# Six buffers for the terms of q, segment ends made in pieces, the first step's loads put ahead, and one-hots made three blocks ahead, in a graph attention layer

## The chip, the cores and the metric

The kernel runs on one core of a Trainium2 chip. A core has TensorE (PE; matmuls and transposes, with weight loads shown apart as PEld), VectorE (DVE), ScalarE (ACT), GpSimd (POOL) and SyncE (SP). SP computes nothing here and issues DMA transfers; POOL issues the indirect ones. Sixteen DMA engines move the data. The metric is the device time of one execution in microseconds; the time of the kernel before is 2341.86 us, the median of three runs (2341.75 to 2342.19).

## The reference

There are 12,500 nodes with 128 features, 212,500 edges sorted by destination, 8 heads of 16. Cut to what is computed:

```python
h = maximum(layernorm(x), 0)
q = h @ Wq.T + bq;  v = h @ Wv.T + bv          # of nodes
k = edge_attr @ Wk.T + bk                      # of edges
in_m   = sum over a head (q[src] * k)
out_m  = sum over a head (q[dst] * k)
diag_m = sum over a head (q[src] * q[dst])
score = (segsoftmax(in_m / 4, dst) + segsoftmax(out_m / 4, dst)
         + segsoftmax(diag_m / 4, dst)) * edge_weight ** lam
agg = segment_sum(score[..., None] * v[dst], dst)
out = x + leaky_relu(agg @ Wo.T + bo, 0.1)
```

## The kernel before

The function `ordered_path` does the work (`general_path` is skipped for these inputs). Edges are cut into blocks of `BE` = 512, and these into five streams of consecutive blocks (`S` = 5). A step `t` takes one block of each stream, so there are `T` = 84 steps and 420 blocks; block `g` is stream `g % 5` of step `g // 5`.

**The stage of the nodes** (0 to 155 us). For 25 groups of up to four tiles of 128 nodes, h is normalized, turned and multiplied by wq (`rectify`, `turn_h`, `nodes_q`), and q is stored to `q_table` in float32 by SP (line 833). Beside it the arrays of the edges are made: source indices (`edges_1`), flags of segment starts (`edges_2`), the position of each edge's destination relative to its block's first one (`edges_3`, `rel_b`, stored to `rel_d`) and the weight in three bf16 terms (`edges_4`), the flags and terms stored to `fa_d` by `fa_out` from the rotating tile `of`. Then POOL starts to gather rows of `q_table` by source index for the first nine blocks (`gather`, line 625, four gathers of 128 rows a block), SP loads the edge features of the first six blocks (`fetch_edges`, line 617), and `terms_q` splits q into three bf16 terms: for group g ACT copies the first term (line 845), DVE subtracts it (846), and one call later ACT makes the second (851), DVE the third (852), and SP stores the tile `q3` to `q3_table` (854). `q3` has three buffers. In the middle of these, after group 12, `edges_5` checks the order of the edges (line 756), marks the ends of segments (758) and turns them (707, 708).

**The loop over the blocks.** For a block the destination's q is not gathered. Edges are sorted, so the destinations of a block lie in a window of 42 nodes: SP loads the window's rows of `q3_table` (`win`, line 1054, an address from a register that SP has loaded from `bases`, 1049) and the relative positions, spread over 126 partitions (`relb`, 1044); ACT makes one-hots of them (`one_hots`, 1062 and 1063), and PE spreads the window's rows over the edges (`spread_q`, 1087). ACT copies the result beside the gathered rows (1089). Edge features are turned (`turn`, 1068 and 1070) and multiplied by wk (`project`, 1076 and 1078), and DVE forms products and sums (`logits`, 1097, 1098, 1100). Scans over the five streams together, in places 0 to 4 of the following steps, give running maxima and sums, from which finished nodes are computed between the blocks (`nodes_between`) or after the loop.

**What sets the order.** Nearly every instruction passes through `pin`, which ties it behind the instruction pinned last on the same engine: the order on an engine is the order of the program. `fetch(t)` loads what step t needs and is called at place 3 of step t - 2; `fetch(0)`, `fetch(1)` and the five one-hots of step 0 stand before the loop. A gather runs `LOOK` = 9 blocks ahead of the loop, into 11 buffers; from block 10 on it also waits for products of PE, by this part of `gather`:

```python
if (g - LOOK, j) in behind:
    tc.add_manual_dep(rows.ins, behind[g - LOOK, j], ...)   # j = 0: project(g - LOOK)
```

Edge features are loaded six blocks ahead into seven buffers, `relb` and `win` have two buffers, and the one-hots of a step one tile of five blocks, in two buffers.

Of the kernel before, what the change touches and what calls it, by code (L numbers as in the profile page):

```python
# [7 lines left out]
F32 = mybir.dt.float32  # L8
BF = mybir.dt.bfloat16
I32 = mybir.dt.int32  # L10
AF = mybir.ActivationFunctionType
# [461 lines left out]
def ordered_path(ctx: ExitStack, tc: tile.TileContext, flag, x, src, dst, edge_attr, edge_weight,  # L473
# [118 lines left out]
    def pin(inst):  # L592

        engine = str(inst.ins.engine)
        if engine in pinned:
            tc.add_manual_dep(inst.ins, pinned[engine], mybir.DependencyInfo(
                mybir.DependencyClass.NoSync, mybir.DependencyReason.DATA), reason="in order")
        pinned[engine] = inst.ins.name
        return inst
# [8 lines left out]
    qqs, st, eas, behind = {}, {}, {}, {}  # L608

    def fetch_edges(g):  # L610
        if g < S * T:
# [37 lines left out]
    with tc.tile_pool(name="prep", bufs=1) as prep, \  # L649
# [49 lines left out]
            nc.gpsimd.tensor_tensor(weight, weight, lam_sb.to_broadcast([RW, RC]), op=ALU.pow)  # L699


        def turn_edges(of, to):
            cols = of.rearrange("r (a p j) -> r a j p", a=RB, j=JN)
            for a in range(RB):
                t_ps = prep_ps.tile([P, JN, RW], F32, name="t_ps")
                for j in range(JN):
                    pin(nc.tensor.transpose(t_ps[:, j, :], cols[:, a, j, :], ident[:RW, :RW]))
                pin(nc.vector.tensor_copy(to[:, a:NB:RB, :], t_ps.rearrange("p j r -> p r j")))
# [8 lines left out]
                                  of.rearrange("r (a e) -> r a e", a=RB)))  # L717

        def of_tile():
            return prep.tile([RW, RC], BF, name="of", bufs=2)  # L720

        def edges_1():
            pin(nc.vector.tensor_copy(src_f, src_r))
# [10 lines left out]
        def edges_3():  # L734
            base_c = prep.tile([RW, RB], F32, name="base_c")
            pin(nc.vector.tensor_copy(base_c, dst_f[:, 1:RC + 1:BE]))
            for a in range(RB):
                part = rel[:, a * BE:(a + 1) * BE]
                pin(nc.vector.tensor_scalar(part, part, base_c[:, a:a + 1], 1.0, op0=ALU.subtract,
                                            op1=ALU.add))  # L740
            rel_b = prep.tile([RW, RB, BE], BF, name="rel_b")
            pin(nc.gpsimd.tensor_copy(rel_b.rearrange("r a (j p) -> r a j p", j=JN),
                                      rel.rearrange("r (a p j) -> r a j p", a=RB, j=JN)))
            pin(nc.sync.dma_start(rel_d.rearrange("(r a) e -> r a e", a=RB), rel_b))
# [5 lines left out]
                pin(nc.vector.tensor_sub(weight, weight, of))  # L750
            fa_out(c + 1, of)

        def edges_5():
            bad = got["bad"] = prep.tile([RW, 1], F32, name="bad")
            step = got["step"]
            pin(nc.vector.tensor_reduce(bad, step[:, :RC], AX.X, ALU.min))
            last = step[:, 1:]
            pin(nc.vector.scalar_tensor_tensor(last, last, 0.0, rel, op0=ALU.is_gt, op1=ALU.mult))
            turn_edges(last, ends)

        def turn_w(i, to):
            w_ps = prep_ps.tile([P, F], F32, name="t_ps")
# [76 lines left out]
        def terms_q(g):  # L839

            if g < GN:
                n = len(tiles_of(g))
                q = xq[:, g * JN:g * JN + n, :]
                q3 = q3s[g] = node.tile([P, JN, 3, F], BF, name="q3", bufs=3)[:, :n]
                pin(nc.scalar.copy(q3[:, :, 0, :], q))
                pin(nc.vector.tensor_sub(q, q, q3[:, :, 0, :]))
            if g > 0:
                n = len(tiles_of(g - 1))
                q = xq[:, (g - 1) * JN:(g - 1) * JN + n, :]
                q3 = q3s.pop(g - 1)  # L850
                pin(nc.scalar.copy(q3[:, :, 1, :], q))
                pin(nc.vector.tensor_sub(q3[:, :, 2, :], q, q3[:, :, 1, :]))
# [36 lines left out]
            gather(g)  # L889
        for g in range(AHEAD):  # L890
            fetch_edges(g)
        for g in range(GN + 1):
            terms_q(g)
            if g == GN // 2:
                edges_5()
        bad = got["bad"]

        found = prep.tile([1, 7], F32, name="found")
# [25 lines left out]
        nc.vector.tensor_copy(flag, found[:, 6:7])  # L924


    fin = ctx.enter_context(tc.tile_pool(name="fin", bufs=2))

    def unit_in(to, u):
# [9 lines left out]
    class Nodes:  # L939
# [88 lines left out]
    with tc.tile_pool(name="work", bufs=2) as work, \  # L1028
            tc.tile_pool(name="scan", bufs=2) as scan, \
            tc.tile_pool(name="ps", bufs=1, space=PSUM) as ps:  # L1030
        ks, eTs, qds, lTs, base_v = {}, {}, {}, {}, {}
        end = S * T

        def block_rows(t):
            lo = t if t < G else t - 1
            return lo, slice(0, S * G) if t < G else slice(1, S * G + 1)

        def fetch(t):

            if t >= T:  # L1040
                return
            at, part = block_rows(t)
            relb = load.tile([K3, S, BE], BF, name="relb")
            pin(nc.sync.dma_start(relb, rel_d[part].rearrange("(s b) e -> s b e", b=G)
                                  [None, :, at, :].to_broadcast([K3, S, BE])))
            fa = load.tile([4 * S, BE], BF, name="fa", bufs=4)
            for s in range(S):
                pin(nc.sync.dma_start(fa[4 * s:4 * s + 4], fa_d[s * G + t]))
            _, base_v[t] = nc.values_load_multi_w_load_instructions(
                bases[0:1, t, 0:S], engines=[mybir.EngineType.SP], min_val=0, max_val=N - 1,  # L1050
                skip_runtime_bounds_check_because="the indices of nodes are below N")
            win = load.tile([K3, S, F], BF, name="win")
            for s in range(S):
                pin(nc.sync.dma_start(win[:, s, :], q3_table[bass.ds(base_v[t][s] * 3, K3), :]))
            st[t] = dict(relb=relb, fa=fa, win=win)

        def one_hots(t, s):

            if s == 0:
                st[t]["oh"] = work.tile([K3, S, BE], BF, name="oh")  # L1060
            d = st[t]["relb"][:, s, :]
            pin(nc.scalar.activation(d, d, AF.Abs, bias=before[:K3]))  # L1062
            pin(nc.scalar.activation(st[t]["oh"][:, s, :], d, AF.Relu, bias=1.0, scale=-1.0))  # L1063

        def turn(g):
            eT_ps = ps.tile([P, JN, P], F32, name="eT_ps", bufs=2)
# [16 lines left out]
        def spread_q(g):  # L1083
            s, d = g % S, st[g // S]
            qd_ps = ps.tile([P, JN, F], F32, name="qd_ps")
            for j in range(JN):
                pin(nc.tensor.matmul(qd_ps[:, j, :], d["oh"][:, s, j * P:(j + 1) * P],  # L1087
                                     d["win"][:, s, :], start=(j == 0), stop=(j == JN - 1)))
            pin(nc.scalar.copy(qqs[g][:, :, 1, :], qd_ps))  # L1089
            qds[g] = qd_ps  # L1090

        def logits(g):
            s, t = g % S, g // S
# [142 lines left out]
                    r.normalize(0, 4)  # L1236

        products = str(mybir.EngineType.PE)
        fetch(0)
        fetch(1)  # L1240
        for s in range(S):
            one_hots(0, s)
        turn(0)
        turn(1)
        spread_q(0)
        project(0)
        for g in range(end + 2 * S):
            s, t = g % S, g // S
            if g < end:
                gather(g + LOOK)  # L1250
                fetch_edges(g + AHEAD)
            if g + 1 < end:
                project(g + 1)
                behind[g + 1, 0] = pinned[products]
                spread_q(g + 1)
            if g + 2 < end:
                turn(g + 2)
            if g < end:
                logits(g)
            if t + 1 < T:  # L1260
                one_hots(t + 1, s)
            if s == 0:
                later(turn_logits, t - 1)
                later(turn_sums, t - 2)
            elif s == 1:
                later(scan_max, t - 1)
            elif s == 2:
                later(to_rows, t - 2)
                later(powers, t - 1)
            elif s == 3:  # L1270
                later(scan_sums, t - 1)
                if t + 2 < T:
                    fetch(t + 2)
            else:
                later(select, t - 1)
                later(put_rows, t - 2)
            behind[g + 1, 2] = pinned[products]
# [72 lines left out]
```

## Time and profile before

| | |
|---|---|
| median of three runs | 2341.86 us |
| the profiled execution, its span | 2333.37 us, 2331.5 us |
| busy: PE, PEld, DVE, ACT, POOL | 78%, 61%, 92%, 65%, 71% of the span |
| gathers (L625, POOL) | 1680, 966 ns each in the mean |
| products and sums (L1097, L1098, L1100, DVE) | 420 each, 677, 1214 and 1753 ns |
| one-hots (L1062, L1063, ACT) | 420 each, 729 and 630 ns |
| first gather; first and last block's L1097 | 91.7; 169.8 and 2260.2 us |

The span is the time from the first instruction of the profiled execution to the last. Busy time leaves out what an engine spends on issue: a gather occupies POOL for its duration and the gap to the next one. In lists of waits a line gives the engine and line that waited, what ended the wait, the sum in us, how often, and the longest. In timelines the columns are start in us, duration in us, engine, line, operation, destination<-sources, shapes, count, and in brackets the engine's idle time before it with what ended that.

### The profile page before, as it was taken

What the parts mean: (1) busy time and instruction counts of PE and PEld (TensorE: products, weight loads), DVE (VectorE), ACT (ScalarE), POOL (GpSimd) and SP (SyncE); (2) the same over time, 40 slices, a digit from 0 to 9 for tenths busy, and PEclk for the clock granted to TensorE, in tenths of its full rate; (3) what the DMA queues carried; (4) which work ended last, traced back from release to release, by engine and by line L of the source; (5) the groups of instructions that cost most, each with busy time, mean ns of one, the idle gap of its engine ahead of it and who ended that gap; (6) DMA issues with size and microseconds to landing.
All of it is one profiled execution on the core that took longest, in us unless ns stands there. A gap on an engine that the chain in (4) does not pass through costs nothing. (4 is left out here: it accounts for less than half of the span.)

```text
span 2331.5 us, 35994 instructions
## 1 busy us (share of the span) xinstructions
PE 1812.6 (78%) x10629; PEld 1415.8 (61%) x10629; DVE 2150.8 (92%) x2263; ACT 1522.1 (65%) x2797; POOL 1658.1 (71%) x1715
## 2 busy tenths in 40 slices
PE   5327888888788888878878778888887777888775
PEld 4315666666666666666666566666666666666654
DVE  7659999999999999999999999999999999999983
ACT  5547676666766676666676676667666667667653
POOL 3547777777777777777777777777777777777740
PEclk9757777777778787787777787778687888688777
DMA  7657545555555555555555655554555554554522
GB/s 201 215 172 197 148 135 148 143 144 149 141 136 159 138 141 163 139 139 154 146 138 139 164 138 140 156 144 137 158 142 140 153 154 135 153 154 134 149 54 60
DMA packets 306681, 341.04 MB, mean 146 GB/s; under 512 B 137667, under 2 KB 225496, under 8 KB 306165
## 3 DMA queue, kind: packets, MB, share of 16 engines
q1 hardware_dynamic: 244906, 222.99, 32.5%
q0 software_dynamic: 54448, 112.96, 19.9%
q10 hardware_dynamic: 7120, 2.70, 0.4%
q8 instruction: 85, 1.39, 0.2%
q14 instruction: 122, 1.00, 0.1%
HBM read 307.79 MB, written 30.64 MB: 145 GB/s over the span
## 5 line engine op out<-in xcount | busy, mean ns | idle before, releaser
L625 POOL DMA_INDIRECT qq<-q_table,src_i x1680 | 1623.4, 966 | 548.6 <-issue 341.4
L1100 DVE TENSOR_REDUCE lT<-prod 128x96 f32<-128x1536 f32 x420 | 736.2, 1753 | 14.4
L1078 PE MATMUL k_ps<-wk,eT 128*128 128x128 f32 x3360 | 613.3, 338 | 103.6 <-ACT eT L1070 95.4
L1078 PEld LDWEIGHTS k_ps<-wk,eT 128*128 128x128 f32 x3360 | 518.9, 236 | 263.7 <-ACT eT L1070 180.9
L1089 ACT COPY qq<-qd_ps 128x512 f32<-128x512 f32 x420 | 245.4, 584 | 548.9 <-PE qd_ps L1087 432.2
L1098 DVE TENSOR_TENSOR prod<-qq,k_ps 128x1024 f32<-128x1024 f32 x420 | 509.8, 1214 | 0.5 <-PE k_ps L1078 0.5
L1087 PE MATMUL qd_ps<-win,oh 126*128 126x128 bf16 x1680 | 203.4, 257 | 213.4 <-DVE prod L1097 173.1
L1068 PE MATMUL eT_ps<-ident,ea 128*128 128x128 f32 x1680 | 342.0, 341 | 2.9 <-DVE found L901 2.9
L1097 DVE TENSOR_TENSOR prod<-qq,qd_ps 128x512 f32<-128x512 f32 x420 | 284.3, 677 | 47.4 <-ACT qq L1089 34.6
L1087 PEld LDWEIGHTS <-oh 126*128 126x128 bf16 x1680 | 159.5, 116 | 257.5 <-issue 208.4
L1062 ACT ACTIVATE relb<-relb,before 126x512 bf16<-126x512 bf16 x420 | 306.3, 729 | 7.4 <-DMA relb<-rel_d 7.4
L1070 ACT COPY eT<-eT_ps 128x512 f32<-128x512 f32 x420 | 246.9, 588 | 50.3 <-PE eT_ps L1068 48.7
L1063 ACT ACTIVATE oh<-relb 126x512 bf16<-126x512 bf16 x420 | 264.6, 630 | 13.4
L1068 PEld LDWEIGHTS eT_ps<-ident,ea 128*128 128x128 f32 x1680 | 243.0, 181 | 3.2 <-DVE found L901 3.2
L1178 PE MATMUL b_ps<-ident,sum 120*128 120x120 f32 x672 | 141.1, 342 | 94.8 <-ACT l L1120 92.3
L1076 PE MATMUL k_ps<-b,ones 3*128 3x512 bf16 x420 | 190.8, 454 | 5.0 <-DVE prod L1098 4.8
L1191 PE MATMUL w_ps<-back,sel 128*126 128x144 f32 x1344 | 186.9, 295 | 0.6 <-ACT back L1179 0.6
L1178 PEld LDWEIGHTS b_ps<-ident,sum 120*128 120x128 f32 x672 | 101.3, 215 | 138.6 <-ACT l L1120 111.4
L1191 PEld LDWEIGHTS w_ps<-back,sel 128*126 128x126 f32 x1344 | 178.4, 197 | 0.8 <-ACT back L1179 0.8
L1179 ACT COPY back<-b_ps 128x480 f32<-128x480 f32 x168 | 97.6, 581 | 47.0 <-PE b_ps L1178 47.0
L1130 DVE TENSOR_TENSOR_SCAN u<-l,u,far_ps 120x512 f32<-120x512 f32 x83 | 105.5, 1271 | 0.8 <-ACT l L1120 0.8
L1158 DVE TENSOR_TENSOR_SCAN sum<-keep,sum,up 120x512 f32<-120x512 f32 x83 | 105.9, 1276 | 0.0
(170 smaller groups left out, 1735.4 us busy)
## 6 DMA issues: line engine op xcount, KB each, us to landing
ea<-in_edge_attr_dram SPq DMA_DIRECT2D x419, 256.0 KB
relb<-rel_d SPq DMA_DIRECT2D x84, 630.0 KB
qq<-q_table,src_i POOLq DMA_INDIRECT x1680
win<-q_table SPq DMA_DIRECT2D x420, 31.5 KB
q_table<-q SPq DMA_DIRECT2D x24, 384.0 KB
fa<-fa_d SPq DMA_DIRECT2D x420, 4.0 KB
sums<-rows SPq DMA_DIRECT2D x416, 7.9 KB
q_table<-xq SPq DMA_DIRECT2D x24, 256.0 KB
```

Of the source, the lines that this page charges most:

```text
L625: rows = pin(nc.gpsimd.indirect_dma_start(out=qq[:, j, 0, :], out_offset=None, in_=q_table, in_offset=bass.IndirectOffsetOnAxis(ap=src_i[: ...
L1062: pin(nc.scalar.activation(d, d, AF.Abs, bias=before[:K3]))
L1063: pin(nc.scalar.activation(st[t]["oh"][:, s, :], d, AF.Relu, bias=1.0, scale=-1.0))
L1068: pin(nc.tensor.transpose(eT_ps[:, j, :], eas[g][:, j * F:(j + 1) * F], ident))
L1070: pin(nc.scalar.copy(eT, eT_ps))
L1078: pin(nc.tensor.matmul(k_ps[:, j, :], eTs[g][:, j, :], wk, start=False, stop=(j == JN - 1)))
L1087: pin(nc.tensor.matmul(qd_ps[:, j, :], d["oh"][:, s, j * P:(j + 1) * P], d["win"][:, s, :], start=(j == 0), stop=(j == JN - 1)))
L1089: pin(nc.scalar.copy(qqs[g][:, :, 1, :], qd_ps))
L1097: pin(nc.vector.tensor_mul(prod[:, :, 2, :], qqs[g][:, :, 0, :], qds[g]))
L1098: pin(nc.vector.tensor_mul(prod[:, :, 0:2, :], qqs[g], ks[g][:, :, None, :].to_broadcast([P, JN, 2, F])))
L1100: pin(nc.vector.tensor_reduce(lTs[t][:, :, s, :], prod.rearrange("p j i (h d) -> p j (i h) d", d=DIM), AX.X, ALU.add))
L1191: pin(nc.tensor.matmul(w_ps[:, i].rearrange("p s c -> p (s c)"), d["sel"][:, j, lo:lo + 3, :].rearrange("p s w -> p (s w)"), d["back"][:, ...
```

## The change

There are four parts. The tile `q3` gets six buffers: four of its own, and for every third group one of the two `of` tiles, for which `rel_b` becomes an `of` tile too. `edges_5` is cut into six pieces, one after every third call of `terms_q`. `fetch` is split: `fetch(t)` loads relb and fa and the registers, `fetch_rows(t)` the windows; both move up in the program, and `fetch(0)` is called before `terms_q`. The one-hots get a tile for each block, in five buffers; one block's are made at a time, three blocks ahead of the loop, and before the loop the first block's one-hots, turn, project and spread_q come ahead of the second block's turn.

```diff
+    def fetch(t):
...
+        relb = load.tile([K3, S, BE], BF, name="relb")
+        pin(nc.sync.dma_start(relb, rel_d[part].rearrange("(s b) e -> s b e", b=G)
+                              [None, :, at, :].to_broadcast([K3, S, BE])))
+        fa = load.tile([4 * S, BE], BF, name="fa", bufs=4)
+        for s in range(S):
+            pin(nc.sync.dma_start(fa[4 * s:4 * s + 4], fa_d[s * G + t]))
+        _, base_v[t] = nc.values_load_multi_w_load_instructions(
...
+    def fetch_rows(t):
...
+        win = st[t]["win"] = load.tile([K3, S, F], BF, name="win")
+        for s in range(S):
+            pin(nc.sync.dma_start(win[:, s, :], q3_table[bass.ds(base_v[t][s] * 3, K3), :]))
...
         def of_tile():
-            return prep.tile([RW, RC], BF, name="of", bufs=2)
+            return prep.tile([P, RC], BF, name="of", bufs=2)[:RW]
...
-            rel_b = prep.tile([RW, RB, BE], BF, name="rel_b")
+            rel_b = of_tile().rearrange("r (a e) -> r a e", a=RB)
...
-        def edges_5():
-            bad = got["bad"] = prep.tile([RW, 1], F32, name="bad")
+        def edges_5(i):
             step = got["step"]
-            pin(nc.vector.tensor_reduce(bad, step[:, :RC], AX.X, ALU.min))
             last = step[:, 1:]
-            pin(nc.vector.scalar_tensor_tensor(last, last, 0.0, rel, op0=ALU.is_gt, op1=ALU.mult))
-            turn_edges(last, ends)
+            if i == 0:
+                bad = got["bad"] = prep.tile([RW, 1], F32, name="bad")
+                pin(nc.vector.tensor_reduce(bad, step[:, :RC], AX.X, ALU.min))
+            elif i == 1:
+                pin(nc.vector.scalar_tensor_tensor(last, last, 0.0, rel, op0=ALU.is_gt,
+                                                   op1=ALU.mult))
+            elif i < 2 + RB:
+                turn_edges(last, ends, [i - 2])
...
-                q3 = q3s[g] = node.tile([P, JN, 3, F], BF, name="q3", bufs=3)[:, :n]
+                if g % 3 == 2:
+                    q3 = prep.tile([P, JN, 3, F], BF, name="q3", tag="of", bufs=2)
+                else:
+                    q3 = node.tile([P, JN, 3, F], BF, name="q3", bufs=4)
+                q3 = q3s[g] = q3[:, :n]
...
         for g in range(AHEAD):
             fetch_edges(g)
+        fetch(0)
         for g in range(GN + 1):
             terms_q(g)
-            if g == GN // 2:
-                edges_5()
+            if g % 3 == 2:
+                edges_5(g // 3)
...
-        def one_hots(t, s):
-
-            if s == 0:
-                st[t]["oh"] = work.tile([K3, S, BE], BF, name="oh")
-            d = st[t]["relb"][:, s, :]
-            pin(nc.scalar.activation(d, d, AF.Abs, bias=before[:K3]))
-            pin(nc.scalar.activation(st[t]["oh"][:, s, :], d, AF.Relu, bias=1.0, scale=-1.0))
+        def one_hots(g):
+
+            if g < end:
+                oh = ohs[g] = work.tile([K3, BE], BF, name="oh", bufs=5)
+                d = st[g // S]["relb"][:, g % S, :]
+                pin(nc.scalar.activation(d, d, AF.Abs, bias=before[:K3]))
+                pin(nc.scalar.activation(oh, d, AF.Relu, bias=1.0, scale=-1.0))
...
-        fetch(0)
+        fetch_rows(0)
         fetch(1)
-        for s in range(S):
-            one_hots(0, s)
+        fetch_rows(1)
+        one_hots(0)
         turn(0)
+        project(0)
+        spread_q(0)
         turn(1)
-        spread_q(0)
-        project(0)
+        one_hots(1)
+        one_hots(2)
...
-            if t + 1 < T:
-                one_hots(t + 1, s)
+            one_hots(g + 3)
...
-                if t + 2 < T:
-                    fetch(t + 2)
+                fetch(t + 2)
+                fetch_rows(t + 2)
```

More of the change, by code (lines that the diff above doesn't have):

```diff
@@ L606, in rows_in, with block_rows @@
         q.dma_start(to[RW - 1:RW, :E - top], t[None, top:E])
-    qqs, st, eas, behind = {}, {}, {}, {}
+    qqs, st, eas, behind, base_v = {}, {}, {}, {}, {}
+    def block_rows(t):
+        lo = t if t < G else t - 1
+        return lo, slice(0, S * G) if t < G else slice(1, S * G + 1)
+    def fetch(t):
+        if t >= T:
+            return
+        at, part = block_rows(t)
+        relb = load.tile([K3, S, BE], BF, name="relb")
[5 more added lines that the diff above has]
+        _, base_v[t] = nc.values_load_multi_w_load_instructions(
+            bases[0:1, t, 0:S], engines=[mybir.EngineType.SP], min_val=0, max_val=N - 1,
+            skip_runtime_bounds_check_because="the indices of nodes are below N")
+        st[t] = dict(relb=relb, fa=fa)
+    def fetch_rows(t):
+        if t >= T:
+            return
+        win = st[t]["win"] = load.tile([K3, S, F], BF, name="win")
+        for s in range(S):
+            pin(nc.sync.dma_start(win[:, s, :], q3_table[bass.ds(base_v[t][s] * 3, K3), :]))
     def fetch_edges(g):
@@ L699, in ordered_path, with turn_edges @@
             nc.gpsimd.tensor_tensor(weight, weight, lam_sb.to_broadcast([RW, RC]), op=ALU.pow)
-        def turn_edges(of, to):
+        def turn_edges(of, to, which=range(RB)):
             cols = of.rearrange("r (a p j) -> r a j p", a=RB, j=JN)
-            for a in range(RB):
+            for a in which:
                 t_ps = prep_ps.tile([P, JN, RW], F32, name="t_ps")
@@ L924, in ordered_path @@
         nc.vector.tensor_copy(flag, found[:, 6:7])
+    assert GN // 3 >= 2 + RB
     fin = ctx.enter_context(tc.tile_pool(name="fin", bufs=2))
@@ L1030, in ordered_path @@
             tc.tile_pool(name="ps", bufs=1, space=PSUM) as ps:
-        ks, eTs, qds, lTs, base_v = {}, {}, {}, {}, {}
+        ks, eTs, qds, ohs, lTs = {}, {}, {}, {}, {}
         end = S * T
[L1034 to L1046, printed above, removed]
-            for s in range(S):
[L1048 to L1055, printed above, removed]
-        def one_hots(t, s):
-            if s == 0:
-                st[t]["oh"] = work.tile([K3, S, BE], BF, name="oh")
-            d = st[t]["relb"][:, s, :]
-            pin(nc.scalar.activation(d, d, AF.Abs, bias=before[:K3]))
-            pin(nc.scalar.activation(st[t]["oh"][:, s, :], d, AF.Relu, bias=1.0, scale=-1.0))
+        def one_hots(g):
[4 more added lines that the diff above has]
+                pin(nc.scalar.activation(oh, d, AF.Relu, bias=1.0, scale=-1.0))
         def turn(g):
@@ L1086, in spread_q @@
             for j in range(JN):
-                pin(nc.tensor.matmul(qd_ps[:, j, :], d["oh"][:, s, j * P:(j + 1) * P],
+                pin(nc.tensor.matmul(qd_ps[:, j, :], ohs[g][:, j * P:(j + 1) * P],
                                      d["win"][:, s, :], start=(j == 0), stop=(j == JN - 1)))
@@ L1090, in spread_q @@
             qds[g] = qd_ps
+            del ohs[g]
         def logits(g):
@@ L1238, in ordered_path @@
         products = str(mybir.EngineType.PE)
-        fetch(0)
+        fetch_rows(0)
         fetch(1)
-        for s in range(S):
-            one_hots(0, s)
+        fetch_rows(1)
+        one_hots(0)
         turn(0)
+        project(0)
+        spread_q(0)
         turn(1)
-        spread_q(0)
-        project(0)
+        one_hots(1)
+        one_hots(2)
         for g in range(end + 2 * S):
```

## The prediction

> **What bounds the kernel now.** I read the page first, then the waits, then the timeline around the start and the end of the edge loop. The page's 40 slices (58.3 us each) suggest VectorE:
>
> ```profile
> DVE  7659999999999999999999999999999999999983
> POOL 3547777777777777777777777777777777777740
> DMA  7657545555555555555555655554555554554522
> ```
>
> From slice 4 on DVE is at nine tenths and POOL at seven. But the page counts no issue time, so the second view is the list of waits (engine and line, what it waited for: us in total, times, longest):
>
> ```profile
> POOL qq L625 <- issue: 341.4, 1120, 0.3
> ACT qq L1089 <- DMA qq<-q_table,src_i: 106.5, 61, 3.0
> POOL qq L625 <- PE k_ps L1078: 43.6, 58, 26.2
> ACT q L845 <- DMA q_table<-q: 33.8, 21, 8.4
> ```
>
> POOL never waits longer than 0.3 us before a gather, except once, 26.2 us; ACT, which copies the spread q into the same tile, waits 106.5 us for gathers. The timeline near the end of the loop shows who leads (start, us, engine, line):
>
> ```profile
> 2246.76 0.94 POOL L625 DMA_INDIRECT qq<-q_table,src_i  x1 [0.30 <-issue]
> 2250.24 0.68 DVE L1097 TENSOR_TENSOR prod<-qq,qd_ps 128x512 f32<-128x512 f32 x1
> 2251.40 0.58 ACT L1089 COPY qq<-qd_ps 128x512 f32<-128x512 f32 x1 [1.94 <-DMA qq<-q_table,src_i]
> 2251.76 0.94 POOL L625 DMA_INDIRECT qq<-q_table,src_i  x1 [0.30 <-issue]
> 2260.24 0.66 DVE L1097 TENSOR_TENSOR prod<-qq,qd_ps 128x512 f32<-128x512 f32 x1
> ```
>
> The last gather (block 419) is issued by 2252.70, and DVE uses it at 2260.24, 7.5 us later, though the program lets gathers run 9 blocks ahead. I subtracted, for each block, the end of its fourth gather from the start of its L1097. This lead is 33.9 us at block 10, 24.9 at 40, 10.0 at 90, and then stays between 5 and 12 to the end. Up to block 90 DVE works off the lead at 4.78 us a block (blocks 40 to 90); after that it goes at the pace of the gathers: 1640 gathers from 173.73 to 2252.70, each 1.268 us with its 0.30 us of issue, 5.07 us a block. **The loop ends when POOL's stream of gathers ends**, and the remaining 78.8 us (2331.5 - 2252.7) follow it. So the time is set by when that stream runs without a hole. Its one hole:
>
> ```profile
> 146.59 0.94 POOL L625 DMA_INDIRECT qq<-q_table,src_i  x1 [0.30 <-issue]
> 155.69 0.54 SPq L1044 DMA_DIRECT2D relb<-rel_d  x1
> 159.46 3.67 SPq L1054 DMA_DIRECT2D win<-q_table  x5
> 161.79 0.72 ACT L1062 ACTIVATE relb<-relb,before 126x512 bf16<-126x512 bf16 x1 [7.41 <-DMA relb<-rel_d]
> 168.84 2.08 PE L1078 MATMUL k_ps<-wk,eT 128*128 128x128 f32 x8 [4.42 <-ACT eT L1070]
> 171.38 2.08 PE L1078 MATMUL k_ps<-wk,eT 128*128 128x128 f32 x8
> 173.73 0.94 POOL L625 DMA_INDIRECT qq<-q_table,src_i  x1 [26.20 <-PE k_ps L1078]
> ```
>
> Forty gathers (blocks 0 to 9) are through at 147.53; gather 41 is tied to the products of block 1 (line 171.38), which come only after the terms of q are stored, the first step is loaded and its one-hots are made. A change here is worth at most 26.2 - 0.3 = 25.9 us, unless the first forty get quicker.
>
> **The terms of q (stores L854).** With three buffers the store of group g holds up L845 of group g + 3:
>
> ```profile
> 102.06 0.62 ACT L845 CAST q<-xq 128x512 bf16<-128x512 f32 x1 [2.04 <-DMA q_table<-q]
> 103.32 0.68 DVE L852 TENSOR_TENSOR q<-xq,q 128x512 bf16<-128x512 f32 x1
> 106.90 0.62 ACT L845 CAST q<-xq 128x512 bf16<-128x512 f32 x1 [1.94 <-DMA q_table<-q]
> ```
>
> L852 ends at 104.0, and its buffer is free at 106.9: a store takes 2.6 to 3.0 us to land in all such pairs. Groups 6 to 12 start 2.38 us apart (103.82 to 118.11), while DMA is only 0.68 busy (100 to 120). In the DMA records a store is 256 packets of 1536 bytes at 66 ns, over 16 engines 1.05 us; a gather is 16 packets at 280 ns, 0.28 us per 1.27. So two stores' latency, not bandwidth, sets this pace. Six buffers leave five stores in flight; then the slower of two limits holds: DMA, 1.05 / (1 - 0.22) = 1.35, and DVE, 0.61 + 0.69 = 1.30 us a group. I take 1.40.
>
> **The loads put ahead** (fetch(0): relb, five fa, the registers). On SP's queue they now stand between the six ea and the first store: 0.54 + 1.93 + 1.33 (the median of the register loads, L1049) = 3.8 us, so that store is issued at 95.3 instead of 91.54. In the DMA engines it also goes behind relb, 630 packets of 1024 bytes at 74 ns = 2.9 us. Before, the first store landed at 97.5; now about 100.5. Behind it waits ACT's L845 of group 6, and behind that everything of the later groups. This is a loss of 3 us on the stage, paid out of 18 gained below.
>
> **The ends in pieces.** Before, L756 (2.28), L758 (2.29) and four turns with copies (2.6, and waits for PE) stood together between 119.97 and 128.5 and starved the stores: DMA was at 0.17 between 124.5 and 129.5. The same instructions now come after groups 2, 5, 8, 11, 14 and 17. The first two fall before the first landing, when DVE has nothing else to do (groups 0 to 5 plus both end near 98); the four copies, 0.6 each, hide behind four queued stores. If that cover were gone they would cost their 7.2 us again.
>
> So the last store lands near 100.5 + 24 x 1.40 = 134, against some 158.4 before (issued 155.65, + 2.8).
>
> **From there to gather 41.** The order is new: one-hots of block 0 (0.72 + 0.63), copy of eT(0) 0.59, project(0) 2.08, spread_q(0) 0.64, copy of qq 0.60, the turn and copy of eT(1) about 1.0, bias and project(1) 2.7: 9 us if even the first one-hot must wait for the last store (its tile may lie in released memory; relb is there). The win loads take 2.5 us beside it. Queued behind these on ACT are one-hots 1 and 2, needed two blocks later; on SP, fetch(1), whose relb is first read in block 2. Project(1) ends near 143. Before, five pairs of one-hots (6.4 us) stood ahead of eT(0).
>
> **The forty gathers.** They end at 147.5, after 143. POOL is then the later one by 4.5 us, and gather 41 follows at 147.8: **25.9 us** earlier. The one operation that might delay them is the denser DVE work. One gather of the old stage is long:
>
> ```profile
> 122.28 2.29 DVE L758 SCALAR_TENSOR_TENSOR step<-step,dst_r 104x2048 f32<-104x2048 f32 x1
> 122.42 2.98 POOL L625 DMA_INDIRECT qq<-q_table,src_i  x1 [0.30 <-issue]
> ```
>
> It took 2.98 instead of 0.944 beside an instruction with two SBUF inputs. The Trainium skill ("SBUF — State Buffer", Who interferes with whom) says that such an instruction and a GpSimd one that reads SBUF exclude each other for a whole instruction. Taken for all of them (50 subtractions of 0.68 plus 2.29 = 36 us) the forty would end at 91.66 + 40 x 1.25 + 36 = 178, and the change would lose 4 us. But the same instructions ran beside the same gathers here: all forty together are 6.2 us over 0.944 each. I keep the row: between 0 and some 10 us over, 141 to 151 for the end.
>
> **The rotation of "of".** rel_b loses its own buffer, so the cast L748 that ran at 73.58 must wait for rel_d's store, issued at 69.37; the next such wait (78.83, for a store issued at 73.21) shows 5.6 us, so to 75.0. Behind it on DVE stand L750 and L832, behind these the last q_table stores and the first gather: 0 to 1.4 us; I take 0.4, since L832's sums have three PSUM tiles of slack.
>
> **One-hots in the loop** number the same, on ACT (65% busy), three blocks ahead instead of five. relb is needed at place 2 of the step before and its buffer is freed at place 1: six blocks, 30 us, for a load that took 6.1 us at the start. Cost 0; rival C prices the other end. The end of the loop and the nodes left over are unchanged.
>
> **Sum.** 25.9 - 0.4 = 25.5 us. The profiled execution took 2333.37 (span 2331.5) and would take 2307.9; the runs' median is 8.5 us above it, and I assume it stays so: 2341.86 - 25.5 = **2316 us**.
>
> **Rivals.**
> A (the forecast, 0.72): POOL's stream is whole; 22 to 29 us, 2313 to 2320.
> B (0.15): the stores don't speed up (receipts, not buffers, are the limit), and PE holds gather 41. At the old 2.38 us the last store lands at 100.5 + 24 x 2.38 = 157.6, project(1) ends at 166.6 and gather 41 starts at 166.9: 7 us, 2335. For it: a store needs 2.6 us with DMA only 0.68 busy. Against it: DMA at 1.02 in another stretch (180 to 195), so more in flight does move more. A pace between gives 2320 to 2335.
> C (0.05, slower): the later relb. If ACT waits for it at place 2 of each of 83 steps, the slack of DVE against POOL, (5.07 - 4.78) x 5 = 1.45 us a step, is used up first; from 1.45 + 25.5 / 83 = 1.76 us a step on the kernel is slower; at 2 us it is 83 x 0.55 - 25.5 = 20 us more, 2362. Against it: 24 of the 30 us would have to be lost.
> D (0.04): no change, within 0.2% (4.7 us, about what a measurement of this kernel can tell). A gather interval longer by 25.5 / 1640 = 16 ns would do it; 2342.
> E (0.04): the stage's delays of gathers (6.2 us) vanish too: up to 32 us, 2310.
>
> **The numbers.** Faster is A, B and E, 0.91; same 0.04; slower 0.05. The range 2311 to 2329 leaves out C, D, the far end of B and of E.
>
> **What would show it.** L845's wait falls from 33.8 us to near 10; stores start about 1.4 us apart; DMA near 0.9 from 95 to 134. POOL has no hole over 5 us; its last gather ends near 2227, and interval and final lead stay 1.268 and about 8 us. A hole before gather 41 means B; waits of ACT's L1062 on relb mean C. The forecast is wrong if gathers are not the bound, that is if their last one moves by 26 us and the end does not.

## The result and the profile after

The changed kernel takes **2318.68 us** (median of four runs, 2315.46 to 2320.5) against 2342.03 us (four runs, 2341.75 to 2345.21) for the kernel before: the ratio on record is 0.9895, with a 95% interval of 0.9881 to 0.991. The gain is 23.4 us by the medians; 2316 us and 25.5 us of gain were predicted. The profiled execution took 2320.5 us (span 2318.7), the longest of its four, while the profiled execution before was 8.4 us or more below the other runs of its kernel, so the two profiles differ by only 12.9 us. Nine of the twelve runs below came on chips where this program, before as after, takes some 2918 us: the instructions of VectorE, ScalarE and GpSimd have the same durations there, but in the loop pauses appear on every engine, many of which no row of the profile explains, and gathers come 1.60 us apart and stay 46 to 60 us ahead of their use.

Lines have moved: the gather is now L652, the terms of q are L880 to L889 (L880 and L881 the first term and its subtraction, L889 the store), the checks and marks of the ends L785 and L787, the one-hots L1076 and L1077, the products L1112 to L1115. The slices of the page (58.0 us each) look like those of before, but for the second and third, where all three rows are fuller (DMA 0.7 and 0.8 for 0.6 and 0.5; the third was where POOL and the stores had stood still):

```profile
DVE  6889999998999999999989999999999999999983
POOL 3677777777777777777777777777777777777750
DMA  7785555454554545555544555555455454545522
```

The list of waits (engine and line, what it waited for: us in total, times, longest):

```profile
POOL qq L652 <- issue: 321.2, 1053, 0.3
ACT qq L1103 <- DMA qq<-q_table,src_i: 76.6, 39, 4.3
DVE prod L1112 <- DMA qq<-q_table,src_i: 17.2, 16, 3.5
ACT q L880 <- DMA q_table<-q: 5.7, 1, 5.7
```

No wait over 0.3 us before a gather is left but that of the first, and L880 waits for a store once, 5.7 us, where L845 had waited 33.8 us. The second and third lines name the DMA landing that came last before a wait ended, and a landing of a later block's gather counts there too; so each wait has to be set against the landings of its own block. By the semaphores of the traces a gather has landed about 2 us after its instruction ends (the median). Counting only waits that ended within 0.3 us of the last landing of the block's own gathers, L1112 waits for gathers 11 times, 13.7 us in all; before the change this was so 3 times, 1.6 us. The timeline shows how the start went (start, us, engine, line; brackets: idle before it and what ended that):

```profile
93.40 7.44 POOL L652 DMA_INDIRECT qq<-q_table,src_i  x1 [10.77 <-DMA ea<-in_edge_attr_dram]
93.99 0.68 DVE L881 TENSOR_TENSOR xq<-xq,q 128x512 f32<-128x512 f32 x1
...
97.08 4.34 SPq L889 DMA_DIRECT2D q_table<-q  x4
97.60 2.28 DVE L787 SCALAR_TENSOR_TENSOR step<-step,dst_r 104x2048 f32<-104x2048 f32 x1
101.14 0.97 POOL L652 DMA_INDIRECT qq<-q_table,src_i  x1 [0.30 <-issue]
102.24 0.62 ACT L880 CAST q<-xq 128x512 bf16<-128x512 f32 x1 [5.71 <-DMA q_table<-q]
...
127.71 0.72 ACT L1076 ACTIVATE relb<-relb,before 126x512 bf16<-126x512 bf16 x1
133.05 2.51 SPq L635 DMA_DIRECT2D win<-q_table  x5
136.99 0.69 DVE L1112 TENSOR_TENSOR prod<-qq,qd_ps 128x512 f32<-128x512 f32 x1 [3.27 <-ACT qq L1103]
137.87 2.08 PE L1092 MATMUL k_ps<-wk,eT 128*128 128x128 f32 x8
151.11 0.94 POOL L652 DMA_INDIRECT qq<-q_table,src_i  x1 [0.30 <-DMA qq<-q_table,src_i]
152.36 0.94 POOL L652 DMA_INDIRECT qq<-q_table,src_i  x1 [0.30 <-PE k_ps L1092]
...
2241.05 0.94 POOL L652 DMA_INDIRECT qq<-q_table,src_i  x1 [0.30 <-issue]
2242.03 0.68 DVE L1112 TENSOR_TENSOR prod<-qq,qd_ps 128x512 f32<-128x512 f32 x1
...
2248.51 0.66 DVE L1112 TENSOR_TENSOR prod<-qq,qd_ps 128x512 f32<-128x512 f32 x1
```

The products of block 1 (137.87) are done 12 us before the fortieth gather ends (152.05), and gather 41 follows at 152.36 without a hole: POOL alone decides when it starts, 21.4 us earlier than before. The first L1112 comes 32.8 us earlier (136.99 for 169.79). But the last gather ends at 2241.99, only 10.7 us earlier. The 1640 gathers between have a mean interval of 1.2744 us instead of 1.2679, and 1640 x 6.5 ns = 10.7 us. The end of the loop follows 6.5 us behind the last gather (7.5 before).

### The profile page after: what moved, and what is told of

It reads as the page before. It is cut to its first block, busy times and chain, and to the rows that moved or that the text cites. A ratio compares the mean times of both kernels' runs of the same rounds, so it can differ in the third digit from the quotient of the medians.

```text
span 2318.7 us, 35998 instructions
## 1 busy us (share of the span) xinstructions
PE 1817.0 (78%) x10629; PEld 1416.8 (61%) x10629; DVE 2150.2 (93%) x2263; ACT 1523.5 (66%) x2797; POOL 1671.1 (72%) x1715
## 5 line engine op out<-in xcount | busy, mean ns | idle before, releaser
L652 POOL DMA_INDIRECT qq<-q_table,src_i x1680 | 1636.4, 974 | 523.0 <-issue 321.2
L1115 DVE TENSOR_REDUCE lT<-prod 128x96 f32<-128x1536 f32 x420 | 736.1, 1753 | 14.4
L1112 DVE TENSOR_TENSOR prod<-qq,qd_ps 128x512 f32<-128x512 f32 x420 | 284.3, 677 | 62.2 <-ACT qq L1103 41.0
L1076 ACT ACTIVATE relb<-relb,before 126x512 bf16<-126x512 bf16 x420 | 306.3, 729 | 0.0
L1077 ACT ACTIVATE oh<-relb 126x512 bf16<-126x512 bf16 x420 | 264.5, 630 | 17.6 <-DVE flag L960 4.2
```

Of the source, the lines that this page charges most:

```text
L652: rows = pin(nc.gpsimd.indirect_dma_start(out=qq[:, j, 0, :], out_offset=None, in_=q_table, in_offset=bass.IndirectOffsetOnAxis(ap=src_i[: ...
L1077: pin(nc.scalar.activation(oh, d, AF.Relu, bias=1.0, scale=-1.0))
L1112: pin(nc.vector.tensor_mul(prod[:, :, 2, :], qqs[g][:, :, 0, :], qds[g]))
L1115: pin(nc.vector.tensor_reduce(lTs[t][:, :, s, :], prod.rearrange("p j i (h d) -> p j (i h) d", d=DIM), AX.X, ALU.add))
```

## The experiments

Differences are against the changed kernel. The runs on the chips with 2918 us tell of the head of the kernel up to some 130 us, of the forty gathers, and of the gathers' durations. What bounds the loop is told by the last three ("_b"), on a chip where the kernel before takes 2344.08 us; where they are set against the 2318.68 us of the result, 2 us of the difference may be the chip's.

**The pair again.**

> The kernel before, unchanged, for a second profile of it: how much of the difference between two profiles is the execution and not the kernel. If the gathers' interval (1.268 us before, 1.274 us after, over 1640 gathers 10.7 us) is a matter of the execution, this profile may show anything from 1.266 to 1.276 and a span of 2331 to 2341 us; if the change made it longer, it shows 1.268 again. The hole before gather 41 is 25 to 27 us in either case.

> The changed kernel, unchanged, beside the kernel before, for a second profile. If this execution's engines have no pauses of their own in the loop (the kernel before at 2333 to 2345 us): no hole before gather 41, which starts at 147 to 153 us, gathers' interval 1.266 to 1.276 us, 2312 to 2321 us. If the kernel before takes some 2920 us here, as in the eight runs ahead of this one: gathers are not the bound in the loop, their lead stays near 50 us, and the 21 us by which gather 41 starts earlier need not reach the end: 2895 to 2920 us.

Measured: 2921.07 us for the kernel before, with the same head (forty gathers end at 147.62, a hole of 26.6 us, gather 41 at 174.24), and 2910.48 us for the changed one, 0.9973 (0.996 to 0.9986) of the kernel before on its chip: 7.7 us of gain where 23.4 were had. In after_again the fortieth gather ends at 152.71, but gather 41 waits for PE's products until 160.09. The pauses stand above all in front of PE's products with wk; this is the list of waits of before_again:

```profile
PE k_ps L1078 <- issue: 392.0, 143, 7.9
POOL qq L625 <- PE b_ps L1178: 228.6, 72, 5.1
```

In the first profile PE stood idle for 103.6 us before these matmuls, 95.4 of them for ACT's copies. With POOL held back by PE, an earlier gather stream is worth little. What makes PE pause was not found; its granted clock was lower, 0.702 against 0.777.

**Three buffers for q3, everything else changed.**

```diff
-                if g % 3 == 2:
-                    q3 = prep.tile([P, JN, 3, F], BF, name="q3", tag="of", bufs=2)
-                else:
-                    q3 = node.tile([P, JN, 3, F], BF, name="q3", bufs=4)
+                q3 = node.tile([P, JN, 3, F], BF, name="q3", bufs=3)
```

> The changed kernel with three buffers for the terms of q again, all else as changed. Theory (two stores' latency sets the pace of the terms, and gather 41 waits for what follows them): groups start 2.3 to 2.4 us apart, the last store lands near 157, a hole of 11 to 17 us opens again before gather 41, and the time is 2329 to 2336 us. Rival (the moved loads and the shorter chain to block 0 alone close the hole): under 2322 us.

> The same kernel as three_buffers, taken again. Where the kernel before takes some 2342 us and gathers are the bound: gather 41 after a hole of 11 to 17 us, and 2329 to 2336 us in all, the hole carried to the end of the kernel. Where it takes some 2918 us: again within 0.2% of the kernel before.

Measured: groups 2.4 to 2.5 us apart in both runs, a hole of 16.6 us on the first chip, with 2921.58 us (1.0006, 0.999 to 1.0021), and on the last **2334.92 us**, 0.9964 (0.9932 to 0.9997) of the kernel before. The list of waits and the timeline of three_buffers_b:

```profile
ACT q L877 <- DMA q_table<-q: 34.1, 18, 11.0
```

```profile
147.64 0.95 POOL L652 DMA_INDIRECT qq<-q_table,src_i  x1 [0.30 <-issue]
...
163.16 2.08 PE L1089 MATMUL k_ps<-wk,eT 128*128 128x128 f32 x8
165.51 0.94 POOL L652 DMA_INDIRECT qq<-q_table,src_i  x1 [16.93 <-PE k_ps L1089]
```

With three buffers the first term waits 34.1 us for stores, as before the change (33.8), and gather 41 waits for PE again. It starts 13.2 us later than in the changed kernel, and the median is 16.2 us higher. So the buffers carry some 13 to 16 us of the 23.4, the rest the new order: even with three buffers gather 41 comes 8.2 us earlier than before (173.73 to 165.51), and on its own chip this kernel is 9.2 us faster than the kernel before.

That these microseconds reach the end by the gathers is not shown by this run. Its gathers came a little closer together (1.2690 us), and the last one ends at 2246.34, only 4.3 us later than in the changed kernel. From block 90 on the lead is 6.7 to 18.8 us, 14.2 in the median, and no L1109, as L1112 is called here, waits for a gather of its own block. VectorE began 25.3 us later (162.29 for 136.99) and went at its own pace, 5.046 us a block, against 5.076 for four gathers. The head of the kernel puts off the start of both streams.

**The selection of ends left out in all steps but the first** (L1182, 1025 ns; sums then go to the rows of step 0's ends):

```diff
         def select(t):
-            sel = work.tile([P, JN, S, W], F32, name="sel")
+            if t > 0:
+                st[t]["sel"] = last["sel"]
+                return
+            sel = last["sel"] = scan.tile([P, JN, S, W], F32, name="sel", bufs=1)
```

> The changed kernel without the selection of segment ends in all steps but the first (L1182, two SBUF inputs, 1.03 us): the ends of step 0 are used for every step, so sums go to wrong rows and the work of 83 selections, 85 us of DVE, is left out. Theory (gathers are the bound and L1182 costs them 27.6 us): 2287 to 2297 us, gathers' durations in the loop are 25 to 30 us shorter in all, their interval 1.256 to 1.259. Rival (DVE is the bound): 85 us less, 2234 us. Rival (gathers are the bound but are not held up by DVE): 2316 to 2321 us.

> The selection of ends is left out in all steps but the first (the output is not the reference's); the same kernel as no_sel, taken again to see the loop on a chip where the kernel before takes some 2342 us, if there is one. There: if the gathers are the bound, only their lengthening beside the selection goes (20 to 28 us), and 2287 to 2297 us result; if VectorE were the bound, its 1.3 us of selection a step and more would go, 2234 us or less. Where the kernel before takes some 2918 us: again 2920, with gathers' excess in the loop near 16 us.

Measured: 2920.13 us (1.0014, 1.0001 to 1.0027), and on the last chip **2292.24 us** (0.9773, 0.9745 to 0.9802), 26.4 us below the changed kernel. The groups of gathers on the page, of the changed kernel and of no_sel_b (count; busy us, mean ns; idle before):

```profile
L652 POOL DMA_INDIRECT qq<-q_table,src_i x1680 | 1636.4, 974 | 523.0 <-issue 321.2
```

```profile
L652 POOL DMA_INDIRECT qq<-q_table,src_i x1680 | 1611.7, 959 | 523.0 <-issue 311.6
```

DVE's busy time fell by 76.5 us (2150.2 to 2073.7), but the gathers after the fortieth lost only 25.0 us (their sum over 0.944 us each went from 41.4 to 16.4), and that is about what the time lost. The last gather ends at 2214.81, 27.2 us earlier than in the changed kernel, of which 1.9 us come from the head, and the last L1112 starts 7.4 us after it. POOL has no hole, and L1112 waits for gathers of its own block 24 times, 25.8 us. In these two kernels the gathers' stream sets the end, and one of DVE's instructions acts on the time through the gathers that it lengthens.

**One more product on VectorE in each step**, with one operand in PSUM (dve_psum) or both in SBUF (dve_sbuf), each 1.22 us:

```diff
+            if s == 0:
+                pin(nc.vector.tensor_mul(prod[:, :, 0:2, :], qqs[g],
+                                         ks[g][:, :, None, :].to_broadcast([P, JN, 2, F])))
```

```diff
+            if s == 0:
+                more = work.tile([P, JN, 2, F], F32, name="more_dve", bufs=1)
+                pin(nc.vector.tensor_mul(more, qqs[g], qqs[g]))
```

> The changed kernel with one more product on DVE in every step: the second product of block 0 of the step is made twice (1.21 us, one input in PSUM and one in SBUF; 84 times 102 us of DVE). Theory (gathers are the bound; DVE has 1.2 to 1.5 us a step to spare): less than 15 us more than the changed kernel, 2317 to 2334 us, and the last gather within 10 us of its place. Rival (DVE, 93% busy, is the bound): 102 us more, 2420 us.

> The changed kernel with one more DVE product in every step that has both inputs in SBUF and writes a tile that nothing reads (1.2 to 1.4 us, 84 times). Theory (as for the extra product from PSUM, but an instruction with two SBUF inputs also holds gathers up, as L1182 does: 27.6 us over 84 of them at 1.03 us): gathers' durations grow by 25 to 60 us in all, and the time is 20 to 60 us over that of the run with the input in PSUM. Rival (what holds long gathers up is not DVE's second SBUF input): the two runs are within 5 us.

> The same kernel as dve_psum (one more product of 1.2 us a step on VectorE, with an operand in PSUM), taken again. Where the kernel before takes some 2342 us: 2317 to 2334 us if the gathers are the bound and VectorE has its slack of 0.3 us a block, 1.45 a step; 2420 if VectorE is the bound. Where it takes some 2918 us: again near 2917.

Measured, both on one chip: 2917.11 us (0.9994, 0.9983 to 1.0005) and 2893.23 us (0.9927, 0.9903 to 0.9951; why more work came out faster there is open). The gathers by groups, of dve_psum and of dve_sbuf:

```profile
L652 POOL DMA_INDIRECT qq<-q_table,src_i x1680 | 1634.7, 973 | 1071.9 <-issue 475.8
```

```profile
L652 POOL DMA_INDIRECT qq<-q_table,src_i x1680 | 1664.0, 990 | 1025.8 <-issue 484.1
```

Taking both operands from SBUF costs POOL 29.3 us in 84 instructions, 0.35 us each; the same length of work with an operand in PSUM does not (the gathers after the fortieth sum to 39.6 us over 0.944 each in dve_psum, to 38.3 in after_again and to 69.4 in dve_sbuf).

On the last chip dve_psum_b took **2369.96 us**, 51 us above the changed kernel: this missed both numbers, neither hidden nor paid in full. Its timeline at the end:

```profile
2252.07 0.94 POOL L652 DMA_INDIRECT qq<-q_table,src_i  x1 [0.30 <-issue]
...
2298.43 0.66 DVE L1112 TENSOR_TENSOR prod<-qq,qd_ps 128x512 f32<-128x512 f32 x1
```

Here the last gather is 45.4 us ahead of its use: DVE has become the bound. The slack that I took for it was wrong. In this run DVE is idle for 44 of the 2000 us between 200 and 2200 (86 in the changed kernel), and blocks 100 to 410 take 5.191 us each; less the added 1.22 / 5 = 0.244 that is 4.947 for its own work, against the 5.086 us of a block in the changed kernel. The slack is at most 0.14 us a block, 0.7 us a step; by three_buffers_b, where DVE waits for ACT and PE but for no gather, it is 0.03 us a block. I had read 4.78 us from blocks 40 to 90. By groups, DVE of dve_psum_b between 2000 and 2200 us has lines that have no instruction between 200 and 400 us, the finished nodes:

```profile
L1045 DVE SCALAR_TENSOR_TENSOR h<-h 128x512 f32<-128x512 f32 x3 | 2.1, 692 | 2.5 <-ACT h L1044 2.5
L1046 DVE TENSOR_TENSOR x_in<-h,x_in 128x512 f32<-128x512 f32 x3 | 2.1, 692 | 0.1
L1014 DVE RECIPROCAL ab<-ab 128x96 f32<-128x96 f32 x2 | 1.5, 754 | 0.1
L1034 DVE TENSOR_TENSOR h<-node_ps,score 128x512 f32<-128x512 f32 x2 | 1.4, 692 | 0.4 <-PE node_ps L1029 0.4
```

With four smaller lines they are 8.8 us in 38 blocks, 0.23 us a block that the early stretch doesn't have. In the kernel before, the first of them comes at block 93, just where the lead stops falling; DVE's busy time goes there from 4.65 us a block (40 to 90) to 4.87 (140 to 190).

The wait of ACT for gathers, which the prediction had also read as a sign of who leads, stands in this run too:

```profile
ACT qq L1103 <- DMA qq<-q_table,src_i: 58.6, 28, 3.0
```

Here every gather has landed at least 17 us before its L1112, so this row counts landings of later blocks' gathers and shows no bound.

**The head in the old order**, with six buffers and pieces kept: the loads of the first step after the terms, five one-hots and both turns ahead of the first products.

```diff
-        fetch(0)
         for g in range(GN + 1):
             terms_q(g)
...
+        fetch(0)
         fetch_rows(0)
...
-        one_hots(0)
+        for g in range(S):
+            one_hots(g)
         turn(0)
-        project(0)
-        spread_q(0)
         turn(1)
-        one_hots(1)
-        one_hots(2)
+        spread_q(0)
+        project(0)
...
-            one_hots(g + 3)
+            if g + 3 >= S:
+                one_hots(g + 3)
```

> The changed kernel with six buffers and ends in pieces, but the first step's loads behind the terms again, five blocks' one-hots first, and both turns before spread_q(0) and project(0). Theory (POOL's stream is whole, so the chain behind the last store has some 10 us to spare): project(1) ends at 147 to 153 us, no hole over 2 us before gather 41, 2316 to 2322 us, like the changed kernel. Rival (each part brings its own share, and the shorter chain brings 10 us): 2326 to 2330 us.

Measured: 2911.54 us (0.9979, 0.996 to 0.9998). The stores start at 92.14 instead of 97.08, L880 waits for one only 2.4 us, while DVE still has L787 to run, and the terms end about 4 us earlier. But the forty gathers end at 169.07, not at 152 (151.42 in three_buffers and 152.48 in whole_ends, both on this chip). The timeline of POOL, and below it three lines of DVE's:

```profile
92.29 11.47 POOL L652 DMA_INDIRECT qq<-q_table,src_i  x1 [10.93 <-DMA ea<-in_edge_attr_dram]
104.06 3.69 POOL L652 DMA_INDIRECT qq<-q_table,src_i  x1 [0.30 <-issue]
108.05 3.79 POOL L652 DMA_INDIRECT qq<-q_table,src_i  x1 [0.30 <-issue]
112.14 3.80 POOL L652 DMA_INDIRECT qq<-q_table,src_i  x1 [0.30 <-issue]
116.25 8.69 POOL L652 DMA_INDIRECT qq<-q_table,src_i  x1 [0.30 <-issue]
125.24 1.34 POOL L652 DMA_INDIRECT qq<-q_table,src_i  x1 [0.30 <-issue]
```

```profile
102.72 0.58 DVE L735 COPY ends<-t_ps 128x416 f32<-128x416 f32 x1
106.83 0.58 DVE L735 COPY ends<-t_ps 128x416 f32<-128x416 f32 x1
124.05 0.25 DVE L936 TENSOR_REDUCE found<-t_ps 1x1 f32<-1x104 f32 x1
```

While DVE runs L881, L887 and L787 without a gap, all with two SBUF inputs, POOL gets through five gathers in 33 us. Each of them ends 0.9 to 1.0 us, its own length, after DVE comes to an instruction without two SBUF inputs: the four copies of turned ends from PSUM (102.72, 106.83, 110.94 and 115.05) and L936. So a gather that has met such a run is held to the run's end. In the changed kernel DVE waits 3.0 us for L880 after L787, which ends at 99.88; the first gather ends at 100.84, and from there a gather and one or two instructions of DVE take turns. DVE loses nothing by it: groups 6 to 24 start 23.45 / 18 = 1.30 us apart, and 1.30 in old_head too. I had booked the loads put ahead as a loss of 3 us; the delay that they bring to the stores is also what lets POOL in. That the 17 us would show in the time on a chip like that of the result was not measured.

**The ends in one piece** (after group 12), and **the ends earlier** (its first two pieces in the stage of the nodes):

```diff
-            if g % 3 == 2:
-                edges_5(g // 3)
+            if g == GN // 2:
+                for i in range(2 + RB):
+                    edges_5(i)
```

```diff
-                17: lambda: edges_4(1), 20: lambda: edges_4(2)}
+                17: lambda: edges_4(1), 20: lambda: edges_4(2), 22: lambda: edges_5(0),
+                23: lambda: edges_5(1)}
...
-                edges_5(g // 3)
+                edges_5(2 + g // 3)
```

> The changed kernel with the ends of segments made in one piece after group 12, six buffers kept. Theory: DVE loses 7 to 10 us in the middle of the terms, which the ten spare microseconds before gather 41 cover; the first gather is no longer held by L787's two SBUF inputs and takes 4 to 5 us instead of 7.4, one in the middle takes 3. Hole under 2 us, 2315 to 2322 us. Rival (the pieces are what keeps the stores going): a hole of 5 us or more, 2324 to 2328 us.

> The changed kernel with the first two pieces of the ends (L785, 2.28 us, and L787, 2.29 us, which has two SBUF inputs) put into the stage of the nodes, after groups 22 and 23, and the four turns after groups 2, 5, 8 and 11 of the terms. Theory (POOL's stream is whole from the first gather on, so only its start and its long gathers count): the first gather takes 2 to 4 us instead of 7.4, gather 41 starts 3 to 5 us earlier, 2312 to 2317 us. Against that: the first gather itself may start up to 2 us later, if DVE's 4.6 us delay the last stores of q. Rival (the time follows DVE's work before the loop): no change, 2318 to 2321 us.

Measured: 2908.14 us (0.9961, 0.9947 to 0.9974) and 2915.7 us (1.0005, 0.9985 to 1.0025). In one piece the forty gathers end at 152.47 as in the changed kernel (152.05), the windows are loaded at 137.78 instead of 133.05 and the first product comes at 142.90 instead of 136.99, still ahead of POOL. About 5 us of the 7.2 that I priced for lost cover are there, and POOL hides them: block 1's products end at 149.25. Gather 41 follows after a pause of 2.8 us, where less than 2 were expected; its cause is not in the profile. The time isn't worse than that of after_again (0.9973), though on these chips that says little. With earlier ends the first gather starts at 95.74 (93.40 in the result, 94.61 in after_again) and the forty end at 156.18: no gain. The first gather is short in both runs, 1.32 and 1.33 us, as expected, but another one further on now meets an unbroken run of L881 and L887 and takes 8.31 us (at 126.63) and 9.52 us. This is that of ends_early:

```profile
121.60 9.52 POOL L652 DMA_INDIRECT qq<-q_table,src_i  x1 [0.30 <-issue]
```

## Why the prediction was right

**What bounds the kernel: right for the changed kernel, half right for the one before.** Gathers that got 25.0 us shorter made the kernel 26.4 us faster, and 76.5 us less of DVE work made no more (no_sel_b). A hole put back into the stream came back as time (three_buffers_b), but there VectorE, which had begun later too, was the last. I had read the bend of the lead at block 90 as DVE catching up with the gathers. It is also where the finished nodes begin, and in the kernel before L1097 waited for gathers of its own block only 3 times, 1.6 us. There the two streams went at nearly the same pace and ended 7.5 us apart; from the old start and at three_buffers_b's 5.046 us a block, VectorE would have ended no earlier however whole POOL's stream was (an estimate). The gain came because the new head moved the first product as well, by 32.8 us, more than gather 41's 21.4; then POOL's stream became the later one. The prediction does not count that second start, so to this extent its number was luck.

**The terms of q: right.** 1.40 us a group was forecast, 1.30 measured, at a DMA share of 1.00 from 95 to 115 us and 0.97 from 115 to 130 (0.9 forecast). The landing of the first store was put at 100.5 and came by 102.2, the last one at 134 and came by 133.05, when the windows were loaded. Rival B is refuted: receipts are not the limit once buffers are there. With three buffers a hole is there.

**From there to gather 41: right, with cover to spare.** Project(1) was put at 143, and ended near 140: the first one-hot need not wait for the last store (127.71).

**The forty gathers: the step that was off.** They were to end at 147.5, between 141 and 151; they ended at 152.05. Of the 4.5 us, 1.7 lie in a later first gather (93.40 for 91.66; the delay is there at 65 us already, before the first instruction that the change moves, and in no_sel, no_sel_b, dve_psum, dve_sbuf and after_again, with the same head, the first gather starts anywhere from 91.15 to 94.61, so this is scatter; the rotation of "of" cost nothing: its cast waits 2.4 us for DVE as before), and 2.9 in longer gathers: 9.0 us over 0.944 each instead of 6.2, of which 6.5 in the first one alone. I set the row against the rule of the Trainium skill ("SBUF — State Buffer", Who interferes with whom) and kept the row. The row held here by the order of the work more than by itself, which was luck: the rule puts the end at 178, old_head shows 169.07, and the changed kernel 152.05, where DVE has to wait at the start. The rule speaks of one instruction; here a gather was held over whole runs of them, 9.52 us in ends_early, and where DVE had paused first the two took turns.

**The loop: the term that was taken as fixed.** The interval was to stay at 1.268. It was 1.2744 in this profile, and 1.2690 in three_buffers_b; the gathers' excess over 0.944 us in the loop was 31.2 us before, 41.4 after, 32.8 in three_buffers_b. Most of it sits beside DVE's instructions with two SBUF inputs: 63 gathers beside L1182 carry 27.6 us of it and 42 beside L1148 8.2 us, before the change 50 with 20.7 and 37 with 7.3. How often they meet depends on how the two streams fall against each other. That this also makes the scatter between runs of one kernel (2315.5 to 2320.5) fits, but was only argued. By the profiles the last gather came at 2242 and not at 2227, 4.5 us from the forty and 10.7 from the interval; by the medians, over runs most of which weren't profiled, the gain was 23.4 us and the forecast 2.7 us low.

**One-hots: right** (no wait of L1076 for relb), so C did not come. But its threshold was wrong: with at most 0.7 us of slack a step instead of 1.45, a wait of 0.7 + 25.5 / 83 = 1.0 us a step would have been enough to undo the change, not 1.76. The mechanism of D came in part, 6.5 of its 16 ns. E did not: the delays of gathers in the stage grew.

## What to carry to other kernels

Where a stream of many equal instructions on one engine sets the end, subtract for each use the end of its producer: a lead of a few microseconds says that this stream ends last, when the busy shares point at another engine. That the other engine really waits for it has to be read use by use; two streams can keep a short lead because they happen to go at one pace. Measure an engine's own pace in the stretch where all of its work is present, or by adding a known piece of work to it and reading the new pace: the early blocks here flattered DVE by half of its slack or more. When a wait of one engine is removed, look at who was let in while it waited.

## What the runs showed of the hardware

An indirect gather, 0.944 us alone, took 7.44 to 11.47 us beside an unbroken run of VectorE instructions with two SBUF inputs, while that run kept its 0.68 us an instruction, and ended 0.9 to 1.0 us after the run; beside single ones in the loop it became 0.2 to 0.4 us longer in the mean. The same product with one input in PSUM left the gathers alone (29.3 us of difference over 84 of them). And the same program took 2342 to 2344 us where the result and the last three runs were taken and some 2918 us on three other chips, with nearly the same durations of VectorE, ScalarE and GpSimd instructions (the sums L1100 1753 ns on both), a granted clock of 0.702 for 0.777, and 392 us of pauses before PE's products with wk; the cause is open.
